# Splitting GpSimd's residual sums of elu into one piece per pair of graphs, in a kernel whose instruction order is planned

## The chip, the cores and the metric

The kernel runs on one core of a Trainium2 chip. The core has a matrix engine (TensorE, PE in the profile, with its weight loads as PEld), a vector engine (VectorE, DVE), an engine for activation functions (ScalarE, ACT), a general engine (GpSimd, POOL) and an engine that here only issues DMA transfers (SyncE, SP). Each engine takes its instructions one after the other in its own list; they wait for each other through semaphores. The metric is the device time of one execution in microseconds, the median of three runs. The kernel before takes 1431.12 us (1428.45 to 1432.41).

## The reference

The input x holds 128 graphs of 64 nodes with 256 features; adj holds their edges. Four layers follow on each other. Each normalizes its input, applies relu and adds its result to x:

```python
# layers 0 and 1: graph attention with 4 heads and with 1 head
h = jnp.maximum(_layernorm(x, axis=-1), 0.0)
x = x + _L0_gnn_ref(h, adj, L0_gnn_W, ...)      # ends with jax.nn.elu(...)
h = jnp.maximum(_layernorm(x, axis=-1), 0.0)
x = x + _L1_gnn_ref(h, adj, L1_gnn_W, ...)      # ends with jax.nn.elu(...)
# layer 2: relational convolution; only the one relation "1" occurs in these edges
h = jnp.maximum(_layernorm(x, axis=-1), 0.0)
x = x + _L2_gnn_ref(h, nodemask, adj, ...)
# layer 3: gated recurrence, three steps of m = h @ weight[i]; aggr = A^T m; h = gru(aggr, h)
h = jnp.maximum(_layernorm(x, axis=-1), 0.0)
x = x + _L3_gnn_ref(h, adj, L3_gnn_weight, ...)
```

Everything is in float32. The additions `x = x + elu(...)` of layers 0 and 1 are the residual sums that this document is about.

## The kernel before

Two graphs of 64 nodes fill the 128 partitions, so a pair of graphs is one column block of 256 features. Four pairs (G = 4) make a group, and there are NG = 16 groups. While the recurrence of one group runs, which is the larger part of TensorE's work, the attention and relational layers of later groups are fitted in between.

The residual sum of an attention layer stands at the end of `elu_add`. The tile `o` is the attention's output, `src` the group's part of x (`xg` in the profile), `em` a temporary that shares its place with other tiles and is called `hn` in the profile:

```python
def elu_add(work, src, o, engine, by_scalar=False):
    em = work.tile(list(o.shape), F32, name="em")
    ...
        nc.vector.tensor_scalar(em, o, 0.0, None, op0=ALU.min)
        nc.scalar.activation(em, em, AF.Exp)
    nc.vector.scalar_tensor_tensor(em, em, -1.0, o, op0=ALU.add, op1=ALU.max)
    engine.tensor_tensor(src, src, em, ALU.add)
...
    # in attention(); the first group's sums are VectorE's, all others GpSimd's
    o = aggregate_graphs(pool, psum, t, wv, heads, g < 16)
    elu_add(pool, src, o, nc.vector if g < 1 else nc.gpsimd, g < 0)
```

The next layer's norm reads `src` pair by pair (`bn_stats`, st and mv in the profile), then turns the normalized rows with a block transposition on VectorE and sixteen small transfers (`hT<-hn`).

Within an attention layer, the exponentials `fs` are turned by TensorE (`tp<-ident,fs`), copied to `fT`, sent to DRAM as `row` and read back over all partitions as `t`. VectorE multiplies and bounds `t` (by gd, fd and mt), and TensorE multiplies it with the values (`mm<-wh,t`, `mn<-wh,t`):

```python
pt = psum.tile([P, T], F32, name="tp")
nc.tensor.transpose(pt[:nh, :P], fs.rearrange("p g h -> p (g h)"), ident)
...
nc.vector.tensor_copy(fT, pt[:nh, :P])
row = dram.tile([2, nh * N], F32, name=f"row{layer}")
nc.sync.dma_start(row.rearrange(...), fT.rearrange(...))
for half in range(2):
    nc.sync.dma_start(t[half * N : (half + 1) * N]..., row[half : half + 1, :].to_broadcast([N, nh * N]))
...
    nc.vector.tensor_tensor(t[:, c], t[:, c], flat(gd, c), ALU.mult)
    nc.vector.tensor_tensor(t[:, c], t[:, c], flat(fd, c), ALU.max)
    nc.vector.tensor_tensor(t4, t4, edges, ALU.min)
```

The recurrence keeps its gates in the banks ry, rm, rz, nh and ni; VectorE, ScalarE and GpSimd take them from there, and each bank is used again many times. Its elementwise steps, with the names of the profile:

```python
def r_there(self, h):                       # cut
    nc.scalar.activation(r, y, AF.Tanh, ...)
    nc.vector.scalar_tensor_tensor(t, r, 1.0, t, op0=ALU.add, op1=ALU.mult)       # t<-r,t
def n_there(self, h):
    nc.vector.tensor_tensor(t, t, self.banks["ni"][:, h], ALU.add)
    nc.scalar.activation(t, t, AF.Tanh, ...)
    nc.gpsimd.tensor_tensor(self.d[:, h], self.hT[:, self.c, h], t, ALU.subtract) # d<-hT,t
def m16_there(self):
    nc.scalar.copy(self.z[:, S0], self.banks["ry"][:, S0])                        # z<-ry
def z_there(self, h):
    nc.vector.tensor_tensor(z, self.banks["rz"][:, S0], z, ALU.add)
    nc.scalar.activation(z, z, AF.Tanh, ...)
def h_there(self, h):
    nc.vector.scalar_tensor_tensor(d, self.z[:, h], 1.0, d, op0=ALU.add, op1=ALU.mult)         # d<-z,d
    nc.vector.scalar_tensor_tensor(self.hnew[:, self.c, h], d, 0.5, self.t[:, h], ...)         # hT<-d,t
```

GpSimd also forms sums and differences of the states (`hS`, `aS`) that TensorE multiplies.

None of this runs in the order of the text. A planner (`Plan`) records every operation with an assumed duration, and lists them anew by due times. An operation becomes ready `LATENCY` ns after one of another engine; due times go back from the end of a job, either in proportion or by a factor `spread`; each group's recurrence has a start of its own, `period` us after the last one. For VectorE and GpSimd it keeps the time until which either holds the common port. In the ramp (the first 115 us of the plan) it fills planned pauses of TensorE with products on a constant tile (`ni<-warm`). Each engine then runs its list in order, with true waits. Nearly all lines of the profile have one line number, L388, the place where the planner's calls are made; the groups are told apart by their tiles.

```python
class Job:
    ...
        self.spread = 1.86
class Plan:
    LATENCY = 170.8
...
start, period = 87.96, 83.9
...
    elif g == 2:
        units = [(0, G, (74.5, 120.77, 176.8, 238.5))]
    else:
        end = start + g * period - 32.8
        units = [(0, G, [end - 53.2 * i + x for i, x in ((3, 0.0), (2, -0.95), (1, -4.68), (0, 0.0))])]
```

Of the kernel before, what the change touches and what calls it, by code (L numbers as in the profile page):

```python
# [11 lines left out]
ALU = mybir.AluOpType  # L12
# [8 lines left out]
G = 4  # L21
# [27 lines left out]
class View:  # L49


    def __init__(self, base, shape, steps=(), region=None, live=None):
        self.base, self.shape, self.steps, self.region, self.live = base, tuple(shape), steps, region, live
# [83 lines left out]
class Pool:  # L137
# [25 lines left out]
    def released(self, tag, base, before):  # L163
# [3 lines left out]
        if before < 0:  # L167
            return 0.0
        return sorted(b.end for b in live if not b.left)[before] + Plan.LATENCY

# [29 lines left out]
class Job:  # L200
# [2 lines left out]

    def __init__(self, start, end, after):
        self.start, self.end, self.after, self.left, self.length = start, end, after, 0, 0.0
        self.spread = 1.86


class Plan:

    LATENCY = 170.8

    def __init__(self, nc):
        self.nc, self.on, self.ops, self.job = nc, False, [], None
# [51 lines left out]
    def emit(self):  # L268
# [20 lines left out]
        for op in reversed(self.ops):  # L289
            if op.job.end is None:  # L290
                op.due = 1e9
                for t in op.then:
                    late = 0.0 if t.engine == op.engine else self.LATENCY
                    op.due = min(op.due, t.due - op.job.spread * (op.cost + late))
# [8 lines left out]
        def enter(op):  # L303
            t = 0.0
            for other, data in op.after.items():
                late = other.end + self.LATENCY
                if other.engine == op.engine and not (other.dma and data):
# [137 lines left out]
def kernel(  # L445
# [28 lines left out]
    nc = Plan(tc.nc)  # L474
# [141 lines left out]
    def elu_add(work, src, o, engine, by_scalar=False):  # L616

        em = work.tile(list(o.shape), F32, name="em")
        if by_scalar:
            nc.scalar.activation(em, o, AF.Relu, scale=-1.0)  # L620
            nc.scalar.activation(em, em, AF.Exp, scale=-1.0)
        else:
            nc.vector.tensor_scalar(em, o, 0.0, None, op0=ALU.min)
            nc.scalar.activation(em, em, AF.Exp)
        nc.vector.scalar_tensor_tensor(em, em, -1.0, o, op0=ALU.add, op1=ALU.max)
        engine.tensor_tensor(src, src, em, ALU.add)

    def block_diagonal(dst, src, scalar, op):

# [322 lines left out]
    with ExitStack() as s1:  # L952
# [64 lines left out]
        def load_group(g):  # L1017
            nc.begin(("load", g))
            xg = work.tile([P, G, D], F32, name="xg", bufs=6)
            n = 2 if g == 0 else G  # L1020
            for p in range(0, G, n):
                nc.sync.dma_start(xg[:, p : p + n], xr[:, g * G + p : g * G + p + n, :])
            at = work.tile([P, G // 2, 2, N], I32, name="at", bufs=3)
            for a in range(2):
                for u in range(G // 2):
                    edges = tr[g * G // 2 + u, a]
                    nc.sync.dma_start(at[a * N : (a + 1) * N, u], edges)
            AT.append(at)
            XG.append(xg)
# [71 lines left out]
        def attention(g, p0, n, layer, heads, we, pool):  # L1101
# [49 lines left out]
            for q in range(0, n, m):  # L1151
# [5 lines left out]
# [4 lines that stand above are left out]
        def first_weights():  # L1161
# [84 lines left out]
        def before(g):  # L1246
            ABD[g] = work.tile([P, G, N], F32, name="abd")
            START[g] = before_recurrence(W[3], psum, XG[g], AG[g], ABD[g], g >= AHEAD)

        def recur(g):  # L1250
            recurrence(
                W[3], psum, START.pop(g), XG[g], ABD[g],
                lambda h, part: nc.sync.dma_start(outr[:, g * G : (g + 1) * G, :][part], h[part]),
                g == NG - 1,
            )
# [3 lines left out]
        nc.begin("weights", 18.0, 0 or None)  # L1259
        later_weights(early)  # L1260
        layers = (first_layer, second_layer, third_layer)
        start, period = 87.96, 83.9
        users = {}
        for g in range(NG):
            if g > 1:
                load_group(g)

            if g == 0:
                units = [(0, 2, (-2.5, 24.3, 61.4, 71.1)), (2, 2, (-2.7, 25.3, 58.8, 74.4))]
            elif g == 1:  # L1270
                units = [(0, 2, (24.1, 54.4, 87.6, 97.3)), (2, 2, (45.5, 67.3, 98.2, 128.1))]
            elif g == 2:
                units = [(0, G, (74.5, 120.77, 176.8, 238.5))]
            else:
                end = start + g * period - 32.8
                units = [(0, G, [end - 53.2 * i + x for i, x in ((3, 0.0), (2, -0.95), (1, -4.68), (0, 0.0))])]
            for p0, n, at in units:
                spare = g == 0 and p0 > 0
                for i in range(3):
                    end = None if g < 2 else at[i + 1]  # L1280
                    nc.begin((g, p0, i), at[i], end, [users[i]] if i in users and not spare else [])
                    if g > 1:
                        nc.job.spread = 3.0
                    if not spare:
                        users[i] = (g, p0, i)
                    layers[i](g, p0, n, spare)
            if g == 0:
                nc.begin("make")
                nc.note("-", make_gru, 0.0, [], [], [op for op in nc.ops if any(b.pool is early for b in op.bases)])
            at = start + g * period  # L1290
            nc.begin(("before", g), at - (13.0 if g == 0 else 21.1), at, [("recur", g - 2)] if g > 1 else [])
            before(g)
            nc.begin(("recur", g), at, at + period)
            recur(g)
# [58 lines left out]
    def general_attention(X):  # L1353

        with ExitStack() as s3:
# [16 lines left out]
            for layer, heads, we in ((0, H, w0e), (1, 1, w1e)):  # L1372
                pool = Plain(str(layer))
                gh = G * heads
                with tc.For_i(0, NP, G) as p0:
# [40 lines left out]
                    for c in range(0, gh, 4):  # L1416
# [3 lines left out]
                        nc.vector.tensor_copy(ec[:, c : c + 4, :].rearrange("p h i -> p (h i)"), pt)  # L1420
                    o = aggregate(pool, psum, lambda p, h: ec[:, p * heads + h, :], wv, heads)
                    elu_add(pool, src, o, nc.gpsimd)
                    nc.sync.dma_start(X[:, bass.ds(p0, G), :], src)

# [115 lines left out]
```

## Time and profile before

| what | before |
|---|---|
| time, median of 3 runs | 1431.12 us |
| span of the profiled execution | 1428.7 us |
| granted TensorE clock, mean | 0.997 |
| GpSimd: differences d<-hT,t, 128x256 | 192 of 754 ns |
| GpSimd: residual sums of 128x512 | 4 of 1264 ns |
| VectorE idle until t<-row landed | 95.3 us, 24 times |
| DMA, mean over the span | 48 GB/s |

A span is the time from the first to the last instruction. A group's row reads: line, engine, operation, out<-in by tile names, shape, count, then the busy time in us and the mean ns of one, and after the second bar the idle time of that engine just before and what ended it. TensorE's products overlap and their ends are modelled, so its busy time is a little too high and short waits can be hidden in it; a float32 product is two records in the trace. Idle time of an engine matters only where TensorE, or the last output, waits for it in the end.

### The profile page before, as it was taken

Reading aid. Unit: us, or ns where it says so; the run is one execution under the profiler, and the core shown is the slowest. Engines: PE = TensorE matmul, PEld = TensorE weight load, DVE = VectorE, ACT = ScalarE, POOL = GpSimd, SP = SyncE. Lnnn points to the kernel's source line nnn. Section 1 sums busy time; section 2 is a strip of 40 time slices with the busy share of each in tenths; the row PEclk is TensorE's granted clock in tenths of the full one; section 3 lists DMA queues with packets and bytes.
Section 4 is the critical chain, followed back from the end, with each engine's and each line's share of the span. In section 5 each row is a group of like instructions: output and inputs, shape, how many; then the busy total and the mean of one; then the engine's idle time right before and its main releaser. Section 6 shows DMA issues by size and latency. Waiting matters only on the chain.

```text
span 1428.7 us, 27951 instructions
## 1 busy us (share of the span) xinstructions
PE 1403.0 (98%) x9703; PEld 964.6 (68%) x9703; DVE 1027.9 (72%) x2553; ACT 808.1 (57%) x2045; POOL 600.5 (42%) x744
## 2 busy tenths in 40 slices
PE   9999999999999999999999999999999999999997
PEld 8666666767667666766766676676667666666664
DVE  6658677785958869685886968688686958665544
ACT  3665556565555655655565565556556555554543
POOL 1454344445424444543444354344435434352422
PEclk9999999999999999999999999999999999999998
DMA  8010222222223122222312222231212122111000
GB/s 219 22 20 20 42 60 37 59 44 41 61 49 71 32 63 42 45 60 49 72 31 63 42 46 60 48 72 30 59 28 44 45 45 54 26 22 28 16 15 18
DMA packets 299420, 67.89 MB, mean 48 GB/s; under 512 B 274696, under 2 KB 297480, under 8 KB 299272
## 3 DMA queue, kind: packets, MB, share of 16 engines
q1 hardware_dynamic: 298712, 65.50, 22.0%
q8 instruction: 80, 1.31, 0.4%
q14 instruction: 68, 0.56, 0.1%
q10 hardware_dynamic: 560, 0.52, 0.1%
HBM read 28.06 MB, written 8.53 MB: 26 GB/s over the span
## 4 chain that ended last, share of the span: by engine, by line
PE 88%; DVE 5%; ACT 2%; DMA 2%; SPq 1%; issue 1%; POOL 1%; DVEq 0%; ACTq 0%; POOLq 0%
PE ry L388 22%; PE mm L388 16%; PE rz L388 11%; PE ni L388 10%; PE nh L388 10%; PE rm L388 5%; PE tp L388 4%; PE mm L609 3%; PE tp L609 3%; PE ni L1322 2%; DVE t L388 1%; DMA t<-row 1%; SPq L388 1%; DVE d L388 1%; DVE hT L388 1%
## 5 line engine op out<-in xcount | busy, mean ns | idle before, releaser
L388 POOL TENSOR_TENSOR d<-hT,t 128x256 f32<-128x256 f32 x192 | 143.2, 754 | 485.1 <-ACT t L388 479.8
L388 PE MATMUL ni<-aT,wc 128*128 128x512 f32 x384 | 194.6, 595 | 0.0
L388 PE MATMUL nh<-hT,whh 128*128 128x512 f32 x384 | 193.6, 597 | 0.0
L388 DVE SCALAR_TENSOR_TENSOR t<-r,t 128x256 f32<-128x256 f32 x192 | 110.9, 582 | 66.2 <-ACT r L388 43.4
L388 ACT ACTIVATE z<-z,brz 128x256 f32<-128x256 f32 x192 | 96.8, 504 | 90.4 <-DVE z L388 90.2
L388 ACT COPY z<-ry 128x256 f32<-128x256 f32 x192 | 70.9, 369 | 130.3 <-PE ry L388 86.8
L388 POOL TENSOR_TENSOR hS<-hT 128x256 f32<-128x256 f32 x96 | 79.4, 833 | 121.6 <-PE ry L388 84.5
L388 PE MATMUL ry<-hS,wsum 128*128 128x256 f32 x384 | 117.3, 387 | 2.6 <-ACT z L388 2.6
L388 PE MATMUL rz<-hS,whh 128*128 128x256 f32 x384 | 117.5, 388 | 2.2 <-DVE z L388 2.1
L388 ACT ACTIVATE hn<-xg,var,rstd 128x256 f32<-128x256 f32 x200 | 107.4, 594 | 13.1 <-DVE var L388 12.7
L388 PE MATMUL mm<-wl,hT 128*128 128x512 f32 x248 | 114.7, 597 | 0.1
L388 PE MATMUL ry<-aS,wsum 128*128 128x256 f32 x384 | 114.5, 380 | 0.0
L388 PE MATMUL rz<-aS,wc 128*128 128x256 f32 x384 | 114.4, 380 | 0.0
L388 DVE SCALAR_TENSOR_TENSOR hT<-d,t 128x256 f32<-128x256 f32 x192 | 110.8, 593 | 4.3 <-ACT fd L388 0.5
L388 DVE SCALAR_TENSOR_TENSOR d<-z,d 128x256 f32<-128x256 f32 x192 | 101.1, 537 | 17.2 <-ACT z L388 10.5
L388 ACT ACTIVATE t<-t,bi 128x256 f32<-128x256 f32 x192 | 93.9, 502 | 29.2 <-DVE t L388 28.8
L388 DVE TENSOR_TENSOR t<-t,gd 128x512 f32<-128x512 f32 (+2 forms) x48 | 29.8, 645 | 107.8 <-DMA t<-row 95.3
L388 DVE TENSOR_TENSOR z<-rz,z 128x256 f32<-128x256 f32 x192 | 80.0, 417 | 34.3 <-ACT z L388 17.4
L388 PEld LDWEIGHTS ry<-hS,wsum 128*128 128x128 f32 x384 | 69.4, 190 | 44.5 <-issue 25.3
L388 POOL TENSOR_TENSOR aS<-aT,aS 128x256 f32<-128x256 f32 x96 | 74.0, 772 | 57.8 <-ACT aT L388 57.7
L388 DVE BATCH_NORM_STATS2 st<-xg 128x6 f32<-128x256 f32 x256 | 93.3, 408 | 2.7 <-DMA xg<-in_x_dram 2.7
L388 POOL TENSOR_TENSOR hS<-hT,hS 128x256 f32<-128x256 f32 x96 | 74.7, 778 | 43.9 <-DVE hT L388 43.0
(205 smaller groups left out, 3268.9 us busy)
## 6 DMA issues: line engine op xcount, KB each, us to landing
hT<-hn SPq DMA_DIRECT2D x896, 32.0 KB
xg<-in_x_dram SPq DMA_DIRECT2D x15, 512.0 KB
out_dram<-hnat SPq DMA_DIRECT2D x15, 512.0 KB
t<-row SPq DMA_DIRECT2D x28, 256.0 KB
at<-in_adj_dram SPq DMA_DIRECT2D x64, 32.0 KB
eg<-in_adj_dram SPq DMA_DIRECT2D x64, 32.0 KB
ag<-in_adj_dram SPq DMA_DIRECT2D x16, 128.0 KB
t<-row SPq DMA_DIRECT2D x28, 64.0 KB
```

Source lines behind the costliest of these rows:

```text
L388: return do(*[real(a) for a in args], **{k: real(v) for k, v in kwargs.items()})
L609: nc.nc.tensor.matmul(*[real(x) for x in product], start=True, stop=True)
L1322: nc.spare = lambda: psum.early and nc.nc.tensor.matmul(pause, warm, warm, start=True, stop=True)
```

## The change

GpSimd's residual sum of a whole unit becomes one instruction per pair of graphs, 128x256 each. GpSimd can then take other work of its list between the pieces, the port that it has in common with VectorE is let go between them, and the layer norm of the first pair can start while later pairs are still summed. Five constants of the planner are changed with it, and the planner makes the order of all engines anew.

```diff
-        self.spread = 1.86
+        self.spread = 1.98
...
-    LATENCY = 170.8
+    LATENCY = 172.92
...
-        engine.tensor_tensor(src, src, em, ALU.add)
+        if engine is nc.sync:
+            nc.sync.dma_start(src, em, accum_op=ALU.add)
+        elif engine is nc.gpsimd and 1:
+            for p in range(0, o.shape[1], 1):
+                ps = slice(p, p + 1)
+                engine.tensor_tensor(src[:, ps], src[:, ps], em[:, ps], ALU.add)
+        else:
+            engine.tensor_tensor(src, src, em, ALU.add)
...
-        start, period = 87.96, 83.9
+        start, period = 87.96, 84.11
...
-                units = [(0, G, (74.5, 120.77, 176.8, 238.5))]
+                units = [(0, G, (74.5, 120.77, 180.67, 238.77))]
...
-                units = [(0, G, [end - 53.2 * i + x for i, x in ((3, 0.0), (2, -0.95), (1, -4.68), (0, 0.0))])]
+                units = [(0, G, [end - 53.2 * i + x for i, x in ((3, 0.0), (2, -0.52), (1, -4.68), (0, 0.0))])]
```

The branch for the sync engine isn't taken; sums of the first group stay whole on VectorE.

## The prediction

> **What bounds the kernel now.** I read the busy times first, then the stages, the matrix engine's waits, and last the one row that the change touches. The page opens with this:
>
> ```profile
> span 1428.7 us, 27951 instructions
> ...
> PE 1403.0 (98%) x9703; PEld 964.6 (68%) x9703; DVE 1027.9 (72%) x2553; ACT 808.1 (57%) x2045; POOL 600.5 (42%) x744
> ...
> PE 88%; DVE 5%; ACT 2%; DMA 2%; SPq 1%; issue 1%; POOL 1%; DVEq 0%; ACTq 0%; POOLq 0%
> ```
>
> The first two lines say that TensorE (PE) has something in flight for 1403.0 of 1428.7 us; the third, the chain that ended last, is 88% TensorE. GpSimd (POOL), whose instructions are split, is at 42%. So the change can bring no more than what TensorE loses now, 25.7 us by this count. The view by stages says where (span, then busy us and instruction count of each engine, granted clock, DMA):
>
> ```profile
> 0.00:252.00 252.00, 245.33 (x1767) 173.55 (x1768) 172.76 (x489) 144.70 (x390) 101.59 (x136) 1.00 0.26 60
> 252.00:1092.00 840.00, 837.70 (x5824) 573.64 (x5825) 644.79 (x1567) 488.57 (x1235) 365.93 (x443) 1.00 0.25 51
> 1092.00:1344.00 252.00, 246.58 (x1713) 167.19 (x1712) 170.96 (x409) 138.17 (x338) 108.19 (x132) 1.00 0.18 36
> 1344.00:1428.70 84.70, 73.39 (x403) 50.18 (x402) 39.36 (x89) 36.68 (x84) 24.83 (x34) 0.95 0.05 14
> ```
>
> TensorE is idle for 6.7 us in the ramp, 2.3 us in 840 us of steady state, 5.4 us in the run-down and 11.3 us in the last 85 us, where only the last group's recurrence is left. The waits of TensorE (us in total, times, longest):
>
> ```profile
> PE tp L388 <- DVE hT L388: 3.9, 5, 2.6
> PE ry L388 <- ACT z L388: 3.5, 5, 1.2
> PE ry L388 <- ACT aT L388: 2.7, 3, 0.9
> PE rz L388 <- DVE z L388: 2.1, 6, 0.5
> ...
> PE mm L609 <- DVE t L388: 1.2, 1, 1.2
> ```
>
> No row names GpSimd. They name VectorE and ScalarE, which wait in turn, and there the long sums can stand behind them. The group of the sums, then three VectorE operations of the recurrence with shortest, median and longest duration in ns:
>
> ```profile
> L388 POOL TENSOR_TENSOR xg<-xg,hn 128x1024 f32<-128x1024 f32 x28 | 66.9, 2388 | 18.9 <-DVE hn L388 18.9
> ...
> L388 DVE SCALAR_TENSOR_TENSOR t<-r,t x192: 375/424/2466, 96.0 to 1418.7; 128x256 f32<-128x256 f32 x192
> L388 DVE SCALAR_TENSOR_TENSOR hT<-d,t x192: 394/418/2577, 111.3 to 1422.0; 128x256 f32<-128x256 f32 x192
> L388 DVE SCALAR_TENSOR_TENSOR d<-z,d x192: 384/418/2593, 110.6 to 1421.4; 128x256 f32<-128x256 f32 x192
> ```
>
> The longest of an operation of 0.42 us is as long as one sum. The timeline shows one such case and what it costs:
>
> ```profile
> 1271.11 2.35 POOL L388 TENSOR_TENSOR xg<-xg,hn 128x1024 f32<-128x1024 f32 x1
> ...
> 1271.19 2.55 DVE L388 SCALAR_TENSOR_TENSOR d<-z,d 128x256 f32<-128x256 f32 x1 [0.29 <-POOL d L388]
> ...
> 1273.85 0.37 ACT L388 COPY z<-ry 128x256 f32<-128x256 f32 x1 [2.41 <-DVE d L388]
> ...
> 1274.28 0.70 PE L388 MATMUL ry<-hS,wsum 128*128 128x256 f32 x2 [1.21 <-ACT z L388]
> ```
>
> The sum starts at 1271.11, VectorE's d is drawn out from 0.42 to 2.55 us, ScalarE's copy out of bank ry (it overwrites z) waits for d, and TensorE waits 1.21 us for the bank.
>
> **What the Trainium skill says.** "SBUF — State Buffer", section "SBUF: two separate sides", says that VectorE and GpSimd share one pair of ports by an exclusive lock held for the whole instruction, and that a VectorE instruction with two SBUF inputs takes part against a GpSimd instruction that reads SBUF: whichever starts first makes the other wait to its end. The trace agrees: all three slow operations have two SBUF inputs, and their longest (2466 to 2593 ns) is one sum's 2388 ns plus little. "GPSIMD Engine Reference", section "3.1 Elementwise — side-by-side cycle accounting", gives about 2.6 cycles per element of a two-input operation plus a dispatch cost per instruction. This trace agrees: 2388 ns for 1024 elements and 754 ns for 256 (row d<-hT,t) make 1634/768 = 2.13 ns an element and some 210 ns fixed.
>
> **The change, part by part.** (1) The 28 sums of 128x1024 become 112 pieces of 128x256, the four of 128x512 become eight. A piece should take 754 ns as d<-hT,t does. Four take 3.02 us in place of 2.39, two take 1.51 in place of 1.26: 28 x 0.63 + 4 x 0.25 = 18.6 us more GpSimd time, 600 to about 619 us. It lies beside TensorE; cost on the path: 0.
>
> (2) The lock is let go after each piece. A VectorE operation that meets it waits at most 0.75 us instead of 2.39. If each of the 28 long sums holds up one, VectorE gets back up to 28 x 1.64 = 46 us. It is at 72% and rarely the one TensorE waits for, so nearly all of this is off the path. I looked at each TensorE gap in the timeline for a sum just before it and a drawn-out operation between: 1274.3 us (1.21), 1136.0 us (0.95), 187.4 us (0.75) and 1214.9 us (0.46), together 3.4 us. I count all of it as gained: -3.4 us.
>
> (3) The relisting. Everything is listed anew, for all engines. TensorE gets the same products and two more of the filling products that keep it busy in the ramp: 32.2 us / 242 records, two records each, is 4 x 0.13 = 0.5 us, in a stretch where it would wait anyway; I count +0.3 us. The last 430 or so products of TensorE, some 127 us of work, stand in the same order but for one pair, so the 11.3 us of the tail stay: 0.
>
> (4) The round trip by DRAM. From the fs transposition to the first product of attention, data go out to row, come back as t and pass VectorE. I counted how much TensorE work is listed in between. In layer 0 it was 11.3 us per group in steady state and becomes 12.2; in group 3 it was 11.2 and becomes 16.4. That group's wait, the 1.2 us in the last line of the waits (at 202.4 us), should go: -1.2 us. In layer 1 it was 8.7 us and becomes 8.0, and the trace says that this trip is already late: 9.4 to 10.1 us pass in most groups, and VectorE sits idle for 6 to 7 us until t lands, mostly 6.6 to 7.8 us after the transposition. Taken alone, 0.7 us less work means 0.7 us more wait. Against it stands that the first of the three VectorE products on t took 0.98 instead of 0.42 us there, because GpSimd's aS sums ran beside it, and that these sums now stand earlier. I take 0.1 us lost in each of some nine steady groups: +0.9 us.
>
> Sum: -3.4 + 0.3 - 1.2 + 0.9 = -3.4 us, from 1431.1 to about 1427.5 us. Steady state gains nothing else: the layer norm behind a sum starts there 3.5 to 4.2 us after the sum begins, 1.1 us or more after it ended, since VectorE's list has other work first; and the products fed by it come some 30 us later.
>
> **The rivals.** First, the wait for t takes the place of the one removed: if the layer 1 trip needs its 9.4 us whatever is listed, nine groups lose 0.7 us, 6 us in place of the 0.9 counted, and the change ends near 1433 us. For it speaks that the slack is negative already; against it the earlier aS sums. Second, the new list alone decides: 7000 lines of the listing differ, and TensorE's small losses per group (2.3 us idle in ten groups, and some that the modelled ends of the products hide) can come out better or worse by 0.5 us per group, so 5 us either way, with or without pieces. In favour of the better side: the other constants of the planner changed with it and look tuned (1.98, 172.92, 84.11), which would give about 1422 us. Third, the pieces let VectorE in between, which stretches a sum past 3 us and delays the GpSimd differences d behind it, on which h waits. GpSimd has much idle time ahead of d (485 us in its row), so this would cost about 1 us in all. Fourth, GpSimd or VectorE becomes the bound: at 43% and 72% I rule it out.
>
> **Range and chances.** The most that the waits can give back is 25.7 - 11.3 = 14.4 us, which is 1%, so faster by over 2% (below 1402.5 us) would need TensorE's work itself to shrink, and it doesn't. Slower by over 2% (above 1459.7 us) would need 1.8 us lost in each of 16 groups; the first rival gives 0.7. The 8-in-10 range adds the second rival's 5 us to the first's 1433 above, and below takes 1422 us less 4 for waits that the modelled ends hide: 1418 to 1437 us. That it is faster at all I hold for about two to one. Predicted: 1427.5 us; faster by over 2% 0.01, within 2% 0.98, slower 0.01.
>
> **What would show each step.** Step 1: xg<-xg,hn as 120 pieces at 0.7 to 0.8 us, GpSimd near 619 us. Step 2: the longest t<-r,t, hT<-d,t and d<-z,d near 1.2 instead of 2.5 us, VectorE's busy time some 40 us lower, and no TensorE gap of 1 us behind a sum. Step 3: the last stage again 11 us idle. Step 4: no gap near 200 us on t; VectorE's idle time on t<-row near 95 us, and in steady state 837 us busy of 840. The prediction is wrong if the steady stage loses over 5 us to waits on t in layer 1, or if VectorE's drawn-out operations stay near 2.4 us.

## The result and the profile after

The changed kernel takes 1444.38 us (1443.12 to 1445.22) where the kernel before took 1430.75 us in runs beside it. The ratio is 1.0096, 95% interval 1.0078 to 1.0113: slower by about 1%, 13.6 us. The prediction was 1427.5 us with a range up to 1437 us. The direction was wrong, and the time lies outside the range, though within the 2% to which the prediction gave a chance of 0.98.

The page's opening, the groups of the sums and of VectorE's operations by tile, in the changed kernel:

```profile
span 1441.9 us, 27986 instructions
...
PE 1409.8 (98%) x9707; PEld 967.8 (67%) x9707; DVE 1005.3 (70%) x2553; ACT 810.8 (56%) x2045; POOL 626.6 (43%) x832
...
PE 80%; DVE 14%; ACT 4%; issue 1%; DMA 0%; POOL 0%; SPq 0%; DVEq 0%
...
L388 POOL TENSOR_TENSOR xg<-xg,hn 128x256 f32<-128x256 f32 x120 | 98.6, 849 | 23.0 <-DVE hn L388 23.0
```

```profile
L388 DVE SCALAR_TENSOR_TENSOR t<-r,t x192: 381/425/972, 98.5 to 1431.4; 128x256 f32<-128x256 f32 x192
L388 DVE SCALAR_TENSOR_TENSOR hT<-d,t x192: 375/419/953, 109.2 to 1434.7; 128x256 f32<-128x256 f32 x192
L388 DVE SCALAR_TENSOR_TENSOR d<-z,d x192: 388/425/949, 108.7 to 1434.2; 128x256 f32<-128x256 f32 x192
```

The engine that was to be relieved is relieved: the longest of VectorE's three operations fell from about 2.5 us to under 1 us, and its busy time by 22.6 us. And yet the chain now runs through VectorE for 14%, not 5%, and through TensorE for 80%, not 88%. The stages:

```profile
0.00:252.00 252.00, 244.91 (x1719) 172.29 (x1723) 172.40 (x488) 141.52 (x383) 100.00 (x145) 1.00 0.24 58
252.00:1092.00 840.00, 829.46 (x5756) 566.44 (x5748) 619.95 (x1551) 486.23 (x1214) 383.35 (x498) 1.00 0.24 50
1092.00:1344.00 252.00, 250.15 (x1769) 170.93 (x1768) 169.39 (x420) 140.92 (x353) 109.12 (x143) 1.00 0.19 37
1344.00:1441.90 97.90, 85.31 (x479) 58.13 (x478) 43.56 (x96) 42.08 (x97) 34.16 (x47) 0.97 0.07 18
```

In the steady 840 us TensorE now idles 10.5 us instead of 2.3. That is the new feature, and the waits of TensorE name it:

```profile
PE mm L609 <- PE ry L388: 5.3, 7, 0.9
PE tp L388 <- DVE hT L388: 4.1, 5, 2.6
PE ry L388 <- ACT z L388: 3.4, 6, 1.4
PE rz L388 <- DVE z L388: 3.0, 6, 0.8
PE ry L388 <- ACT aT L388: 1.8, 2, 0.9
PE mm L609 <- issue: 1.7, 1, 1.7
```

The first line puts the wait of mm (the products with t) down to TensorE itself, which is how a wait for several semaphores can read when the true releaser is not the last one seen. The timeline of one group shows the releaser:

```profile
590.28 0.27 PE L388 MATMUL tp<-ident,fs 128*4 128x128 f32 x1
...
592.27 0.45 SPq L388 DMA_DIRECT2D row<-fT  x1
592.76 1.92 SPq L388 DMA_DIRECT2D hT<-hn  x2
...
594.77 1.20 SPq L388 DMA_DIRECT2D t<-row  x2
...
598.12 0.42 DVE L388 TENSOR_TENSOR t<-t,gd 128x256 f32<-128x256 f32 x1 [7.25 <-DMA t<-row]
...
599.32 0.41 DVE L388 TENSOR_TENSOR t<-t,mt 128x256 f32<-128x256 f32 x1
...
599.84 0.40 PE L609 MATMUL mm<-wh,t 64*64 64x257 f32 x1 [0.79 <-PE ry L388]
```

VectorE's last product on t ends at 599.73 us and TensorE starts 0.11 us later, after 0.79 us of waiting. So this is the layer 1 trip by DRAM: 9.56 us from fs to mm, with 8.0 us of work listed in between. In the kernel before, the same stretch of a steady group:

```profile
580.85 0.27 PE L388 MATMUL tp<-ident,fs 128*4 128x128 f32 x1
...
584.31 1.20 SPq L388 DMA_DIRECT2D t<-row  x2
...
590.28 0.43 PE L609 MATMUL mm<-wh,t 64*64 64x257 f32 x1
```

That is 9.43 us, with 8.7 us listed. On the mean of eight steady groups the stretch lasts 9.6 us in both kernels.

Idle time misses waits that the modelled ends of the products hide. For the comparison of all kernels I therefore count TensorE's loss: the time at which a product begins, minus the work begun before it. Work is the spacing of products that follow each other without a wait in the trace of before (0.2155 us for a record of 256 columns, 0.429 for 512), and without the filling products; it is 1327.4 us in every kernel here. The loss in us, by the work done (up to 300 us: ramp; 300 to 1000: steady; from 1000: run-down). Each row, here and below, is one profiled execution, and these lie up to 2.1 us from the median beside them:

| kernel | ramp | steady | run-down | sum | time, us (median) |
|---|---|---|---|---|---|
| before | 48.5 | 22.7 | 24.2 | 95.4 | 1430.75 |
| changed | 54.7 | 33.4 | 19.9 | 108.0 | 1444.38 |

The change lost 6.2 us in the ramp and 10.7 us in steady state, and gained 4.3 us in the run-down. The last 77 us of work lose the same (9.8 and 9.7 us from 1250 us of work on).

### The profile page after: what moved, and what is told of

Its sections match the earlier page's. It is cut to its first block, busy times and chain, and to the rows that moved or that the text cites. A ratio compares the mean times of both kernels' runs of the same rounds, so it can differ in the third digit from the quotient of the medians.

```text
span 1441.9 us, 27986 instructions
## 1 busy us (share of the span) xinstructions
PE 1409.8 (98%) x9707; PEld 967.8 (67%) x9707; DVE 1005.3 (70%) x2553; ACT 810.8 (56%) x2045; POOL 626.6 (43%) x832
## 4 chain that ended last, share of the span: by engine, by line
PE 80%; DVE 14%; ACT 4%; issue 1%; DMA 0%; POOL 0%; SPq 0%; DVEq 0%
PE ry L388 20%; PE mm L388 14%; PE rz L388 10%; PE nh L388 10%; PE ni L388 9%; PE rm L388 5%; PE tp L388 3%; PE mm L609 3%; DVE t L388 3%; PE tp L609 3%; DVE hn L388 2%; DVE st L388 1%; ACT hn L388 1%; DVE d L388 1%; PE ni L1329 1%
## 5 line engine op out<-in xcount | busy, mean ns | idle before, releaser
L388 DVE SCALAR_TENSOR_TENSOR t<-r,t 128x256 f32<-128x256 f32 x192 | 93.5, 488 | 79.0 <-ACT r L388 59.0
L388 POOL TENSOR_TENSOR hS<-hT 128x256 f32<-128x256 f32 x96 | 71.2, 747 | 120.8 <-PE ry L388 85.3
L388 DVE SCALAR_TENSOR_TENSOR d<-z,d 128x256 f32<-128x256 f32 x192 | 99.4, 529 | 24.7 <-ACT z L388 15.1
L388 ACT ACTIVATE t<-t,bi 128x256 f32<-128x256 f32 x192 | 95.0, 502 | 35.6 <-DVE t L388 29.8
L388 POOL TENSOR_TENSOR xg<-xg,hn 128x256 f32<-128x256 f32 x120 | 98.6, 849 | 23.0 <-DVE hn L388 23.0
L388 DVE SCALAR_TENSOR_TENSOR hT<-d,t 128x256 f32<-128x256 f32 x192 | 102.3, 549 | 3.9
L388 DVE TENSOR_TENSOR t<-t,gd 128x512 f32<-128x512 f32 (+2 forms) x48 | 27.6, 599 | 105.4 <-DMA t<-row 92.9
L388 DVE BATCH_NORM_STATS2 st<-xg 128x6 f32<-128x256 f32 x256 | 96.6, 409 | 5.6 <-POOL xg L388 2.9
L388 POOL TENSOR_TENSOR hS<-hT,hS 128x256 f32<-128x256 f32 x96 | 83.0, 864 | 27.1 <-DVE hT L388 26.1
```

Source lines behind the costliest of these rows:

```text
L388: return do(*[real(a) for a in args], **{k: real(v) for k, v in kwargs.items()})
```

## The experiments

My theory after the result: the pieces themselves do what they should, and the list that the planner makes with them costs the time. Three rivals of this theory, other than those of the prediction: A, the pieces cost it by their number; B, within the list, it is the layer 1 trip alone; C, not the pieces but the changed constants (six values on five lines). The code of the edits is shortened. Each time is the median of its runs; ratios are to the kernel before, run beside it.

**Pieces in the old list.** The planner plans one whole sum; when it is emitted, the pieces are written one after the other. All other lists are those of before, instruction by instruction.

```diff
-        engine.tensor_tensor(src, src, em, ALU.add)
+            def pieces():
+                for p in range(o.shape[1]):
+                    s, e = src[:, p : p + 1].real(), em[:, p : p + 1].real()
+                    nc.nc.gpsimd.tensor_tensor(s, s, e, ALU.add)
+            nc.note("Pool", pieces, <cost and port of the whole sum>, [src], [src, em])
```

> The old listing of all engines, unchanged, with each long sum of GpSimd replaced in its place by its pieces. If the pieces themselves cost the time (more GpSimd instructions, more dispatches), this comes near the changed kernel, 1440 us or more. If the new list costs it, this stays at the old time or gains what step 2 of the prediction counted, 1427 to 1431 us, with VectorE's longest d, t and hT near 1.2 in place of 2.5 us.

Measured: 1426.81 us, ratio 0.9977 (0.9968 to 0.9987), 3.2 us faster. The pieces don't cost time; rival A falls. The place that the prediction showed at 1271 us reads now, in the timeline of this kernel:

```profile
1268.68 3.15 POOL L630 TENSOR_TENSOR xg<-xg,hn 128x256 f32<-128x256 f32 x4
1268.75 0.94 DVE L388 SCALAR_TENSOR_TENSOR d<-z,d 128x256 f32<-128x256 f32 x1 [0.28 <-POOL d L388]
...
1269.80 0.37 ACT L388 COPY z<-ry 128x256 f32<-128x256 f32 x1 [0.79 <-PE ni L388]
...
1270.50 0.59 PE L388 MATMUL ry<-hS,wsum 128*128 128x256 f32 x2
```

VectorE's d waits for one piece, 0.94 us in all, and TensorE's product on ry has no wait in brackets any more (it was 1.21 us).

**Whole sums in the new list.** The changed kernel's lists, with one whole sum in the place of the first piece and nothing in the places of the others:

```diff
-                engine.tensor_tensor(src[:, ps], src[:, ps], em[:, ps], ALU.add)
+                def whole(p=p):
+                    if p == 0:
+                        nc.nc.gpsimd.tensor_tensor(src.real(), src.real(), em.real(), ALU.add)
+                nc.note("Pool", whole, <cost and port of one piece>, [src[:, ps]], [src[:, ps], em[:, ps]])
```

> The new listing of all engines, unchanged, with one long sum in the place of the first piece and nothing in the places of the others. If the new list costs the time, this stays near 1444 us or a little above, as VectorE is held up longer (up to 1448). If the pieces cost it, it returns to 1431 us.

Measured: 1473.89 us, ratio 1.0312 (1.0294 to 1.0329). The list, not the pieces, is the worse part, and it is worse still without them. Three of its waits of TensorE, and VectorE's t by tile:

```profile
PE ry L388 <- ACT z L388: 11.1, 21, 1.6
...
PE rm L388 <- DVE hT L388: 4.3, 11, 1.6
...
PE mm L388 <- ACT aT L388: 4.1, 9, 0.5
```

```profile
L388 DVE SCALAR_TENSOR_TENSOR t<-r,t x192: 381/425/2515, 98.9 to 1460.5; 128x256 f32<-128x256 f32 x192
```

As I read it, the new list puts VectorE's work between the pieces in the belief that the port is free there. I had allowed 4 us for that; it is 29.5 us against the changed kernel, about 1 us for each of the 28 long sums. A whole sum also makes the next norm wait longer for its first pair; the two were not told apart.

**An earlier t, by a row written once.** In layer 1 from group 3 on, t is read from a DRAM row that group 3 wrote, in both lists; the results of later groups are then made with group 3's row.

```diff
-                    nc.sync.dma_start(t[...], row[half : half + 1, :].to_broadcast([N, nh * N]))
+                    # listed as before, but emitted with ROW (written in group 3) as the source
+                    transfer(to, of, to.real, kept.real if fixed else of.real)
```

> The new list, but from group 3 on layer 1 reads t from a DRAM row that was written once, in group 3, so that no transfer of t waits for the row of its own group (the result is that of another group's row; the number and size of all transfers stay). If the trip by DRAM in layer 1 sets the steady loss, some 1.0 us in each of about 9 groups comes back: 1434 to 1437 us, and TensorE's waits before mm<-wh,t of layer 1 vanish. If the loss lies elsewhere, it stays within 2 us of 1444.

> The same reading of a row written once, in the old list. If the trip sets the steady loss, the old list has less to gain, as it lists 8.7 us of TensorE work over the trip: 0.3 to 0.5 us in each of about 9 groups, 1426 to 1429 us. If it lies elsewhere: 1431 us.

Measured: 1443.61 us, ratio 1.0100 (1.0083 to 1.0117), and 1429.56 us, ratio 1.0000 (0.9991 to 1.0009): no difference. But the means failed too. In the new list t is still issued 3.7 to 4.6 us after fs (3.7 to 5.4 in the changed kernel) and lands as late, because SyncE issues the transfers hT<-hn that stand before it in its list. This run says that the landing of row is not what the trip waits for; it doesn't say what the trip costs.

**No trip at all.** The transfers of t go to a tile that nobody reads, and VectorE's first product reads a tile loaded once in group 3. All lists stay.

```diff
-                nc.vector.tensor_tensor(t[:, c], t[:, c], flat(gd, c), ALU.mult)
+                # layer 1, from group 3 on; listed as before
+                nc.nc.vector.tensor_tensor(t[:, c], TKEPT, flat(gd, c), ALU.mult)
```

> The new list, unchanged, but from group 3 on VectorE's first product on t in layer 1 reads a tile that was loaded once, in group 3, and the transfers of t go to a tile that nobody reads (so group 3's exponentials stand in for all later groups; number, size and place of all transfers stay). Nothing waits for the trip by DRAM any more. If the trip is the steady loss, TensorE's wait before mm<-wh,t of layer 1, 0.95 us more a group than in the old list, is gone in groups 4 to 12: 8 us less, 1435 to 1437 us. If what it waits for is VectorE's list and not the trip: within 2 us of 1444.

> The same in the old list. There the trip shows itself as TensorE's wait for bank rm behind the products on t, 0.43 us a group: if it is the trip, 9 x 0.43 = 4 us less, 1425 to 1428 us; if not, 1430 us.

Measured: 1439.96 us, ratio 1.0073 (1.0056 to 1.0090), and 1426.66 us, ratio 0.9978 (0.9968 to 0.9988). The line `PE mm L609 <- PE ry` is gone from the waits, so the trip was its cause. But only 4.4 us come back in the new list, not 8, and 3.0 us in the old. The steady loss falls by 5.8 us in the new list (33.4 to 27.6) and by 2.5 in the old (22.7 to 20.2), which would make the trip 3.3 of the 10.7 us lost there. But most of this difference lies where no trip is. The steady loss, divided into the eight stretches from fs to mm and the rest:

| kernel | from fs to mm | rest |
|---|---|---|
| before | 7.6 | 15.1 |
| no trip, old list | 3.9 | 16.3 |
| changed | 12.3 | 21.1 |
| no trip, new list | 8.1 | 19.5 |

Within the stretches the trip gives back 4.2 us in the new list and 3.7 in the old, 0.5 us apart. The rest scatters: in five kernels with the new list it is 19.5 to 22.8 us. So the trip alone explains 0.5 to 3.3 us of the 10.7, and rival B a third of it at most.

**Constants and planning apart.** The pieces planned with the old five constants, and the whole sums planned with the new ones (the two parts of the change's diff, each without the other):

> The pieces as the planner lists them with the old five constants. Its steady list has 8.7 us of TensorE work over the layer 1 trip, as the old one. If the constants cost the time, this is at 1427 to 1432 us. If planning the pieces apart costs it, whatever the constants, 1436 us or more.

> The long sums as the planner lists them with the new five constants. Its steady list has the same 8.7 us over the layer 1 trip and the same distances as the old one. If the constants cost the time: 1438 us or more. If planning the pieces apart costs it: 1428 to 1433 us, with losses in the ramp only.

Measured: 1435.41 us, ratio 1.0043 (1.0026 to 1.0060), and 1435.24 us, ratio 1.0043 (1.0028 to 1.0057). Both lie between the two outcomes that I had expected. Neither part is to blame alone, so rival C falls too: each costs some 5.6 us, both together 13.6. The losses by stage show that these are different losses:

| kernel | ramp | steady | run-down | sum | time, us |
|---|---|---|---|---|---|
| pieces in the old list | 48.2 | 21.3 | 22.5 | 92.0 | 1426.81 |
| whole sums in the new list | 61.3 | 50.4 | 25.3 | 137.0 | 1473.89 |
| no trip, new list | 54.6 | 27.6 | 20.1 | 102.3 | 1439.96 |
| no trip, old list | 49.2 | 20.2 | 23.2 | 92.6 | 1426.66 |
| split, old constants | 57.2 | 22.1 | 20.2 | 99.5 | 1435.41 |
| whole, new constants | 51.2 | 22.3 | 24.6 | 98.1 | 1435.24 |

For the whole sums with the new constants the table shows 2.7 of the 5.6 us: their profiled execution, 1433.73 us, was the fastest of five. Planned with the old constants, the pieces lose no more in steady state than before (22.1) and gain 4 us in the run-down; all of their loss is in the ramp. Of the four combinations of pieces and constants, only the changed kernel, with both, has the bad steady list.

**Pieces apart from group 4 on.** From this follows a kernel: old constants, pieces planned as one up to group 3, apart from there.

```diff
+        elif engine is nc.gpsimd and nc.on and not apart:    # groups up to 3: as in the old list
+            nc.note("Pool", pieces, ...)
         elif engine is nc.gpsimd and 1:                      # groups from 4 on: planned apart
```

> Old constants. Up to group 3 the pieces are planned as one (old list), from group 4 on apart, so the ramp is the old list's and the rest is that of split_old_constants. If that kernel loses its time in the ramp alone, by the loss up to each amount of TensorE work: 48 us after 300 us of work, 22 us more to 1000, 20 us more to the end, 90.6 us in place of the old 95.4: 1425 to 1427 us. If planning apart costs in itself: 1432 us or more.

Measured: 1425.96 us, ratio 0.9967 (0.9955 to 0.9980): the fastest median of all, 4.4 us under the kernel before, as added up. (Loss: 48.6, 21.7 and 21.2 us, sum 91.5.) Against the pieces in the old list the difference, 0.9 us, is not clear.

The same with the new constants:

> The new constants. Up to group 3 the pieces are planned as one, so the ramp is that of whole_new_constants (51 us lost after 300 us of TensorE work, the changed kernel 55), from group 4 on apart, with the steady list of the changed kernel from group 5. If ramp and steady losses belong to the lists of those stretches and add up: 1444.4 - 3.4, 1440 to 1442 us. If the changed kernel's steady loss came from its ramp (a worse phase carried on): 1436 us or less.

Measured: 1443.55 us, ratio 1.0092 (1.0076 to 1.0108). The loss is 53.4, 35.6 and 20.0 us. The ramp gains only 1.3 of the expected 3.4 us, but the high steady loss stays with the steady list, whatever stood before it. It is no phase carried on from the ramp. From 250 us of work on, TensorE's order is that of the changed kernel, and yet the steady loss differs by 2.2 us: so much it can scatter.

**One constant put back**, -0.95 for -0.52, all else as changed:

> The changed kernel with one constant put back, -0.95 for -0.52. Its steady list is another one: 8.7 us of TensorE work over the layer 1 trip, other neighbours. If the steady loss is a matter of which list comes out, it falls from 3.9 to about 2.7 us a group, 9 to 10 us less in all, and with the ramp of the changed kernel or a worse one 1434 to 1438 us. If pieces planned apart cost a steady loss under the new LATENCY and spread, it stays at 1442 us or more.

Measured: 1440.36 us, ratio 1.0073 (1.0058 to 1.0087). Steady loss 25.6 us, 7.8 less, as a new steady list came out; the ramp lost 57.7, 3.0 more; the run-down 20.3. The time lies between the two outcomes expected. Here one small number in the planner changed the losses of two stretches by several us, one up and one down.

**The order of two neighbours.** What else the bad steady list loses can be seen in the same group, some 0.3 us after fs:

```profile
589.56 0.37 ACT L388 COPY aT<-tp 128x256 f32<-128x256 f32 x1 [0.34 <-PE tp L609]
589.93 0.37 ACT L388 COPY mt<-tp 128x256 f32<-128x256 f32 x1
...
590.20 0.38 ACT L388 COPY aT<-tq 128x256 f32<-128x256 f32 x1
...
590.63 0.30 PEld L388 LDWEIGHTS ry<-aT,wc 128*128 128x128 f32 x2 [0.48 <-ACT aT L388]
```

ScalarE copies one half of aT, then the edge bounds mt of another group, then the other half, which TensorE waits for. I changed the last two over, in groups 5 to 13, in the new list and again in the new list without the trip:

```diff
             op.call()       # in the planner's loop: mt's copy is held back until the next call on ScalarE
+            if self.deferred is not None and op.engine == "Activation":
+                self.deferred.call()
```

> The new list with one pair of neighbours on ScalarE changed over in groups 5 to 13: the second half of aT is copied before the edge bounds mt, not after. TensorE's wait for aT behind the fs transposition, 0.25 us a group in the new list, should go: 9 x 0.25 = 2.2 us less, 1441.5 to 1443 us, if the small waits by the order of neighbours are the rest of the steady loss. If such a wait is only passed on to the next one (bank ry, or t): within 1 us of 1444.

> The new list with both: layer 1 of groups 4 on reads a tile loaded once in group 3 (the transfers of t go to a tile nobody reads), and the second half of aT is copied before the edge bounds in groups 5 to 13. If small waits in a row hide each other, so that half_copy_first gained nothing because the wait for t behind it took it over, then without the trip the 0.25 us a group come through: 9 x 0.25 = 2.2 us under no_trip_new_list, 1437 to 1438.5 us. If they are passed on to other waits still: 1440 us.

Measured: 1445.41 us, ratio 1.0101 (1.0083 to 1.0119), and 1437.49 us, ratio 1.0062 (1.0044 to 1.0080). With the trip the swap gains nothing: in the six groups from 5 on, the wait for aT fell from 0.25 to 0.00 us a group, and the one before the products with t rose from 1.05 to 1.24. Without the trip, the steady loss fell from 27.6 to 25.4 us and the median by 2.5 us, but its runs lie from 1434.7 to 1441.9 us, so the trace carries this more than the times. That this is the 2.2 us expected is in part luck: from fs to mm, each of the steady groups now takes 8.40 us and not 9.05, which is 5.2 us less loss in eight (8.1 to 2.9), and the rest lost 3.0 us more in this execution. In these stretches the trip's removal alone gives 4.2 us, the swap alone 1.3 (12.3 to 11.0), both together 9.4. The waits lie in a row, and the later one takes over most of what the earlier one gives.

**Pieces in the list of the new constants:**

> The list of whole_new_constants, unchanged, with the pieces in the places of the long sums. If the pieces themselves save some 3 us whatever the list: 1435.2 - 3.2, 1431 to 1433 us. If that saving belonged to the old list alone: 1435 us.

Measured: 1434.19 us, ratio 1.0028 (1.0018 to 1.0038), where the whole sums in that list had 1.0043 (1.0028 to 1.0057). The intervals overlap: 1 us, perhaps, not 3. What a shorter lock brings is a property of the list too: it takes gaps away only where a sum stood before one.

## Why the prediction was wrong

Step 1 held but for its size: 120 pieces of 849 ns on the mean, not 754, since VectorE's instructions get the port in between; GpSimd is busy for 626.6 us, not 619. Of TensorE's own waits one names GpSimd, for 0.2 us.

Step 2 held in kind, tested alone, and the match of its sum is in part luck. It said -3.4 us; the pieces in the old list brought -3.2. But by the losses 1.4 us of it come in steady state, where the step counted nothing, and 2.0 in ramp and run-down, where it counted 3.4. Of its four gaps, three are gone there (at 187, 1136 and 1274 us); the fourth, 0.46 us at 1215 us, stayed, so that one was not the sum's. VectorE's relief was over-estimated: 30 us in the old list and 23 in the changed kernel, not 46. In the list of the new constants the step brings about 1 us, so -3.2 is no constant of the change either.

The step that failed is step 3, the relisting. I counted +0.3 us, for two filling products, and left all else to the second rival, with 5 us either way. The new list, with the pieces in it, cost 6.2 us in the ramp and, the trip aside, 7.4 to 10.2 us in steady state (10.7 less 3.3 or 0.5), and gave 4.3 us back in the run-down: 9.3 to 12.1 us net. I had compared the two lists at one place in each period, the trip, where TensorE's list can be measured in us of work, and taken the rest as even. The tail was right: its order is unchanged, and so is its loss.

Step 4 was right in kind and too small. The stretch from fs to mm lasts 9.6 us in both kernels, as the prediction's first rival held, and as the listed work fell from 8.7 to 8.0 us, some 0.6 us more is lost in each group (12.3 less 7.6 us in eight), not 0.1. I had counted on GpSimd's aS sums no longer drawing out the first product on t. They don't (0.42 us, not 0.98), but before they did so in three of the nine groups only (0.98, 0.84 and 0.59 us), and SyncE now issues t 3.1 to 5.4 us after fs, where it was 3.0 to 4.4. The prediction's own sign of being wrong came: TensorE's waits on t, seven of them in the first line of its waits, sum up to 5.3 us. Yet the first rival, which I put at 6 us, was half true: it named the trip alone, and without the trip the new list still takes 9.05 us there, 0.65 of them for the order of ScalarE's copies. The wait of group 3 at 202.4 us did shrink, from 1.25 to 0.16 us, but 2 us later TensorE now waits 1.39 us for bank ry; the saving was passed on.

The range was too narrow for the same reason: it took the prediction's second rival, the new list alone, for at most 5 us over the whole kernel, where the kernels that keep the trip differ by 14 us of steady (21.3 to 35.6) and 9.5 us of ramp loss (48.2 to 57.7), the whole sums in the new list left aside. The bound from above, at most 1% to gain, held.

Open: what makes the ramp of the changed kernel lose 6 us. In it, group 3's row is issued right behind a load of 512 KB and t 5.5 us later; this was read, not tested. Runs with one and the same ramp list lose 54.6 to 57.3 us there, so 2 to 3 us of it scatter. And of the 10.7 us in steady state, 4.7 lie between fs and mm, where the trip and the order of ScalarE's copies account for them: with both gone 2.9 us are lost there, in the old list without the trip 3.9. The other 6.0 us lie in the rest of the period, which I haven't taken apart.

## What to carry to other kernels

Where one engine is full and a planner makes the order, test a change of an instruction inside the old order first: here the split alone gains 0.2%, and what the new order did to it was over five times as large and of the other sign. Then compare the two orders in every stretch, ramp, period and run-down, as loss against work: stretches can be joined from different lists, which gave the lowest median here, if not clearly below that of the pieces in the old list. And a wait that is removed in front of a later wait gains little until the later one is gone.

## What the runs showed of the hardware

A VectorE operation with two SBUF inputs that meets a GpSimd sum takes that sum's time on top, and four shorter sums in a row let it in after the first: d took 2.55 us beside a sum of 2.35 us, and 0.94 us beside pieces of 0.8 us. The pieces are drawn out by VectorE in turn, which step 1 left out: with the pieces in the old list, the 91 that begin while a TENSOR_TENSOR or SCALAR_TENSOR_TENSOR of VectorE runs take 0.90 us on the median, the thirteen that meet none 0.72 to 0.73 us.
